# Routing weights stored as the last word of the residual rows, and five sets of expert weights in a fused attention and mixture-of-experts kernel

## The chip, the core and the metric

The kernel runs on one NeuronCore of a Trainium2 chip. Five engines work in parallel, each through its own instructions in order: TensorE (PE in the profile, with its weight loads as PEld), VectorE (DVE), ScalarE (ACT), GpSimd (POOL) and SyncE (SP), which here issues nearly all plain DMAs. Engines wait for each other and for DMAs through semaphores. SBUF is the on-chip memory of 128 partitions, PSUM holds TensorE's results, and HBM lies outside. The metric is the device time of one execution in microseconds (us); lower is better.

## The reference: what is computed

`x` is 2 x 1024 tokens of 256 features in float32. Four layers are added to it in turn, each on a layer norm of `x`:

```python
x = x + cross_attention(layernorm(x), ctx)     # 16 heads over 77 context rows
x = x + head_routed_attention(layernorm(x))    # the 4 best of 16 heads of each batch, 64 wide
x = x + gelu(layernorm(x) @ ctx.T) @ ctx       # per batch, 77 hidden units
x = x + moe(layernorm(x))

def moe(x):                                    # 8 experts, 256 -> 1024 -> 256, top 1
    probs = softmax(x @ w_router)
    sel, wgt = argmax(probs), max(probs)
    out = 0
    for e in range(8):
        y = relu(x @ w1[e] + b1[e]) @ w2[e] + b2[e]
        out = out + ((sel == e) * wgt)[:, None] * y
    return out
```

The change touches the last layer and the memory around it.

## The kernel before

**Tokens and stages.** The 2048 tokens lie as 16 tiles of 128 rows in one SBUF tile `xs`, which is the running `x`. Layers are called "a" (cross attention), "b" (the routed heads), "c" (gelu) and "d" (experts). Every engine's order is the order in which the program is written; `at(stage, step, position, f, ...)` hangs a piece of work on a step of `a_step` or `b_step`, and `piece` puts its copy out of PSUM off to the next step. Layers c and d of the first eight tiles run between the steps of the heads, those of the last eight in `b_end` and in `tail()`, whose `yield n` lets `n` pieces of the expert blocks run in between.

**The heads.** `b_step(i)` computes scores of one query tile against 1024 keys (L783), their maximum (DVE, L800) and exponential (ACT, L807). DVE transposes inside 32 x 32 squares (L813) and SP moves the squares with sixteen DMAs per pair of tiles (`beT<-be`, L835). PE multiplies by the values (L847), four steps later; DVE normalises (L876). The last pair of tiles turns on PE instead (L822).

**Routing.** `d_logits` gives eight logits per token, `d_expert` the best expert and running counts, `d_split` and `d_row` a token's place, `d_probability` the softmax weight of the chosen expert (subtract, exponential on ACT, sum, reciprocal) into `wgt`. Then `d_counts`, `d_blocks` (blocks of 128 rows per expert, and the expert of each block), `d_slots`, `d_tokens` and `d_lists` make the list of rows for each block. This is done twice: for the first eight tiles (five blocks, `K1`), during the heads, and for all the rest, in `tail()`.

**Rows through HBM.** `ztok` in HBM has one row of 513 words per token: 256 of the layer norm `y`, 256 of the residual `xs`, and the weight. `store_rows` stores the first two from SP for a pair of tiles (L337, L338). `store_weights` stores the weights of eight tiles as a column from ACT (L1101): 1,024 single words. `block_rows(n)` gathers a block's 128 rows with an indirect DMA of POOL (L1296) into `zb`, one of five buffers. A gather waits for the stores before it into `ztok`.

**A block.** `block_turn` transposes `y` on PE (`ybps`, L1308), ACT copies it (`ybT`, L1310) and POOL and DVE choose the bias; `block_hidden` runs the first layer (L1328) with relu on ACT (L1334); `block_out` the second (L1342), the bias (DVE, L1349), weight and residual (L1352), and POOL scatters the rows to `out` (L1355). Block `n + 1`'s hidden layer stands before block `n`'s output, and block `n + 2` is turned within it. Twenty blocks run.

**Weights.** `block_loads(n)` reads the expert's number from the table into SP (L1280) and loads `w1s`, `w2s`, `b2s` (L1282, L1286, L1290). There are four sets: one in pool `w0p`, laid on the left side of memory after step 22 of the heads, and three in `w1p`, on the right, where the heads' buffers `ebp` were. Block `n` takes the left set if `n % 4 == 0`. In the loop, block `n + 4` is asked for when block `n` begins; loads of the second table wait until it exists. `qk1`, which holds q, k and v of the second batch, stays to the end.

```python
wp = pools["w", min(n % 4, 1)]
...
next_loads.append(n + 4)
...
with nc.allow_non_contiguous_dma(reason="a column"):
    nc.scalar.dma_start(z[:, :, 2 * D], wgt[:, t0 : t0 + n])
```

Of the kernel before, what the change touches and what calls it, by code (L numbers as in the profile page):

```python
# [9 lines left out]
F32 = mybir.dt.float32  # L10
# [10 lines left out]
P = 128  # L21
# [18 lines left out]
def kernel(  # L40
# [30 lines left out]
    nc = tc.nc  # L71

    B, S, D = x.shape
# [3 lines left out]
    T = B * NT  # L77
# [19 lines left out]
    T1, K1 = 8, 5  # L97
# [14 lines left out]
    ytp = ctx.enter_context(tc.tile_pool(name="ytp", bufs=2, side="right"))  # L112
    ynp = ctx.enter_context(tc.tile_pool(name="ynp", bufs=3, side="right"))
    ap_ = ctx.enter_context(tc.tile_pool(name="ap_", bufs=2, side="right"))
    qk1 = ctx.enter_context(tc.tile_pool(name="qk1", bufs=1, side="right"))
    ybp = early.enter_context(tc.tile_pool(name="ybp", bufs=2))
    wsp = early.enter_context(tc.tile_pool(name="wsp", bufs=1))
    qk0 = early.enter_context(tc.tile_pool(name="qk0", bufs=1))
# [2 lines left out]

    xs = keep.tile([P, T, D], F32, name="xs")
    xv = x.rearrange("b (t p) d -> p (b t) d", p=P)
    ctxs = const.tile([KC, B, D], F32, name="ctxs")
    raw = {
# [203 lines left out]
            )  # L331
        return y

    def store_rows(t0, y_out):

        z = y_out[t0 * P : (t0 + 2) * P, :].rearrange("(t p) d -> p t d", p=P)
        nc.sync.dma_start(z[:, :, :D], rows["d", t0])  # L337
        nc.sync.dma_start(z[:, :, D : 2 * D], xs[:, t0 : t0 + 2, :])  # L338

    def add_bias(t0, n, bias):  # L340
        nc.gpsimd.tensor_tensor(
# [672 lines left out]
    oh = keep.tile([P, T, E], F32, name="eoh")  # L1014
    seen = keep.tile([P, T + 1, E], F32, name="eseen")
    nc.vector.memset(seen[:, 0, :], 0.0)
    wgt = keep.tile([P, T], F32, name="ewgt")
    emx = keep.tile([P, T], F32, name="emx")
    rkhi = keep.tile([P, T], F32, name="rkhi")
    rklo = keep.tile([P, T], F32, name="rklo")  # L1020
# [37 lines left out]
    def d_split(t0, n):  # L1058

        ts_ = slice(t0, t0 + n)  # L1060
        nc.vector.tensor_reduce(rkhi[:, ts_], ranks.pop(t0), AX.X, ALU.add)
        ri = small.tile([P, n], I32, name=f"eri_{t0}", tag=f"eri{n}")
        nc.vector.tensor_copy(ri, rkhi[:, ts_])
        nc.vector.tensor_scalar(ri, ri, P - 1, None, ALU.bitwise_and)
        nc.vector.tensor_copy(rklo[:, ts_], ri)
        nc.vector.tensor_tensor(rkhi[:, ts_], rkhi[:, ts_], rklo[:, ts_], ALU.subtract)
# [19 lines left out]
    def d_probability(t0, n):  # L1086

        ts_ = slice(t0, t0 + n)
        lg = logits[:, ts_, :]
        nc.vector.tensor_tensor(  # L1090
            lg, lg, emx[:, ts_].unsqueeze(2).to_broadcast([P, n, E]), ALU.subtract
        )
        nc.scalar.activation(lg, lg, AF.Exp)
        sm = small.tile([P, n], F32, name=f"esm_{t0}", tag="esm")
        nc.vector.tensor_reduce(sm, lg, AX.X, ALU.add)
        nc.vector.reciprocal(wgt[:, ts_], sm)

    def store_weights(t0, n):
        z = ztok[t0 * P : (t0 + n) * P, :].rearrange("(t p) d -> p t d", p=P)
        with nc.allow_non_contiguous_dma(reason="a column"):  # L1100
            nc.scalar.dma_start(z[:, :, 2 * D], wgt[:, t0 : t0 + n])  # L1101

# [171 lines left out]

    def block_loads(n):
        tab, i = table(n)
        wp = pools["w", min(n % 4, 1)]
        ex = nc.values_load(tab["eidi"][0:1, i : i + 1], engines=SP, min_val=0, max_val=E - 1)  # L1280
        w1s = wp.tile([P, C, F], F32, name=f"w1s_{n}", tag="w1s")
        nc.sync.dma_start(  # L1282
            w1s, w1.rearrange("e (c p) f -> p e c f", p=P)[:, bass.ds(ex, 1), :, :].squeeze(1)
        )
        w2s = wp.tile([P, FC, D], F32, name=f"w2s_{n}", tag="w2s")
        nc.sync.dma_start(  # L1286
            w2s, w2.rearrange("e (c p) d -> p e c d", p=P)[:, bass.ds(ex, 1), :, :].squeeze(1)
        )
        b2s = wp.tile([P, D], F32, name=f"b2s_{n}", tag="b2s")
        nc.sync.dma_start(b2s, b2[bass.ds(ex, 1), :].to_broadcast([P, D]))  # L1290
        ws[n] = (w1s, w2s, b2s)

    def block_rows(n):
        tab, i = table(n)
        zb = ybs[n] = pools["h"].tile([P, ZD], F32, name=f"zb_{n}", tag="zb", bufs=ZB)
        nc.gpsimd.indirect_dma_start(  # L1296
            out=zb[:, :],
            out_offset=None,
            in_=ztok[: T1 * P, :] if n < K1 else ztok[:, :],
            in_offset=bass.IndirectOffsetOnAxis(ap=tab["tok"][:, 0, i : i + 1], axis=0),  # L1300
        )
# [65 lines left out]
    def blocks():  # L1367


        block_turn(0)  # L1370
        block_turn(1)
        yield from block_hidden(0)
        for n in range(used):
            next_loads.append(n + 4)
            loads_due()
            if n + 1 < used:
                yield from block_hidden(n + 1)
            yield from block_out(n, n + 2 if n + 2 < used else None)
            next_rows.append(n + ZB)
            rows_due()  # L1380
# [15 lines left out]
    def every(gen):  # L1396
        for _ in gen:
            pass
# [7 lines left out]
    def at(stage, s, pos, f, *args):  # L1406
        plan.setdefault((stage, s, pos), []).append((f, args))
# [12 lines left out]
    def do_y(tag, t0, eng=nc.vector, store=True):  # L1420
        mv, rs, *y = rows[tag, t0]
        rows[tag, t0] = ln_rows(tag, t0, mv, rs, eng, *y)
        if tag == "d" and store:
            store_rows(t0, ztok)

    def do_rows(tag, t0, bias=None):

# [1 line left out]
        do_y(tag, t0, nc.gpsimd, False)  # L1429
        if bias is not None:  # L1430
            add_bias(t0, 2, bias)

    def store_rows_of(t0):
        store_rows(t0, ztok)

    def do_turn(tag, t0, pool=trp, ptag="tr", later=False):

# [102 lines left out]
    for g in range(3):  # L1540
        s, t0 = 4 * g, TG * g
        at("b", s + 10, 2, do_rows, "c", t0)
        at("b", s + 11, 3, piece, do_turn, "c", t0)
        at("b", s + 12, 3, c_hidden, t0)
        plan_gelu(t0, (s + 13, 0), (s + 13, 0), (s + 13, 2))
        at("b", s + 14, 2, piece, c_out, t0)
        at("b", s + 15, 2, do_rows_act, "d", t0)
        at("b", s + 17, 0, store_rows_of, t0)
        at("b", s + 17, 3, piece, do_turn, "d", t0)
    at("b", 18, 3, piece, d_logits, 0)  # L1550
    at("b", 22, 3, piece, d_logits, 2)
# [8 lines left out]
    plan_gelu(t0, (s + 2, 3), (s + 3, 0), (s + 3, 0))  # L1560
    at("b", s + 3, 2, piece, c_out, t0)
    at("b", s + 4, 2, do_rows_act, "d", t0)
    at("b", s + 5, 3, store_rows_of, t0)
    at("b", s + 5, 3, piece, do_turn, "d", t0)
    at("b", s + 6, 2, piece, d_logits, t0)

# [12 lines left out]
    def part(f, *args):  # L1579
        if f not in gens:  # L1580
            gens[f] = f(*args)
        next(gens[f], None)

    def first_weights():
        part(d_blocks)
        block_loads(0)
# [5 lines left out]


    at("b", 27, 3, d_row, 0, 4)
    at("b", 27, 3, d_probability, 0, 4)
    at("b", 28, 2, d_expert, T1 - 4, 4)
    at("b", 28, 3, lambda: due.append(d_counts(T1, 4)))
    at("b", 29, 2, d_split, T1 - 4, 4)
    at("b", 29, 3, d_probability, 4, 4)
    at("b", 29, 3, store_weights, 0, T1)  # L1600
    at("b", 30, 2, part, d_blocks, T1, K1)
    at("b", 30, 3, d_row, 4, 4)
    at("b", 30, 3, first_weights)
# [4 lines left out]

    def end_1():
        d_tokens(T1, K1)  # L1610
        store_rows_of(t2)
        do_turn("d", t2)

    def end_2():
# [16 lines left out]
    def tail():  # L1631

        do_turn("c", t4)
        yield 2
        do_y("c", t5)
        c_hidden(t4)
        do_power("d", t3)
        gelu(t4)
        yield 2
        do_turn("c", t5)  # L1640
        gelu(t4)
        d_expert(t2, 2)
        yield 2
        c_hidden(t5)
        gelu(t4)
        gelu(t5)
        yield 1
        c_out(t4)
        gelu(t5)
        gelu(t5)  # L1650
        yield 2
        do_power("d", t4)
        c_out(t5)
        do_y("d", t3, nc.gpsimd)
        yield 3
        do_power("d", t5)
        do_y("d", t4)
        yield 2
        do_turn("d", t3)
        do_y("d", t5)  # L1660
        yield 1
        do_turn("d", t4)
        yield 2
        d_logits(t3)
        d_expert(t3, 2)
        d_logits(t4)
        do_turn("d", t5)
        d_expert(t4, 2)
        yield 3
        d_logits(t5, t2, 4)  # L1670
        d_expert(t5, 2)
        d_split(t2, 4)
        yield 5
        evac = d_counts(T, 4)
        d_row(t2, 4)
        yield 1
        evac()
        d_split(t4, 4)
        yield 1
        d_probability(T1, T - T1)  # L1680
        store_weights(T1, T - T1)
        for _ in d_blocks(T, NB - K1):
            yield 2
        loads_due()
        d_row(t4, 4)
        yield 3
        for _ in d_slots(T, NB - K1):
            yield 2
        yield 3
        d_tokens(T, NB - K1)  # L1690
        yield 6
        d_lists(T, NB - K1)
        rows_due()

    with tc.manual_schedule(
# [41 lines left out]
        for s in range(NI):  # L1737
            b_step(s)
            if s == 0:
                a_step(T + 3)  # L1740
            if s == 22:
                early.close()
                pools["r", 0] = ctx.enter_context(tc.tile_pool(name="rp0", bufs=1))
                pools["w", 0] = ctx.enter_context(tc.tile_pool(name="w0p", bufs=1))
                pools["h"] = ctx.enter_context(tc.tile_pool(name="hp", bufs=2))
        b_end(end_1, end_2, end_3, end_4)
        stage_b.close()
        pools["w", 1] = ctx.enter_context(tc.tile_pool(name="w1p", bufs=3, side="right"))
        pools["r", 1] = ctx.enter_context(tc.tile_pool(name="rp1", bufs=1, side="right"))
        for n in range(1, 4):  # L1750
            block_loads(n)
        assert not plan, plan
        pieces = blocks()
# [55 lines left out]
```

## Time and profile before

| | |
|---|---|
| median of 3 runs | 565.71 us (565.46 to 566.82) |
| the profiled execution | 569.74 us |
| its span, first to last instruction | 568.0 us |
| mean granted TensorE clock | 0.966 |
| PE busy | 507.2 us (89%) |
| DVE, ACT, POOL busy | 319.4, 258.7, 195.0 us |
| moved by DMA | 94.33 MB, mean 166 GB/s |

The profile shows one execution. Its page cuts the span into 40 slices of 14.2 us; a digit is the busy share of an engine in tenths:

```profile
PE   3999999879889988899989889779898799999993
DVE  5558677861568977768867977845663111111111
PEclk9969999989987999999999999998999899999998
DMA  8100000020066668776876687578968999999900
```

Up to about 170 us the layer "a" runs, then the heads to about 390 us, and from there the expert blocks: PE is full, DVE nearly idle and the DMA engines busy. The blocks' first slices, near 390 to 450 us, still hold the second half's layers c and d.

In rows of the profile, `out<-in` names what an instruction writes and reads, `xN` how many there are, and `L1296` is a line of the kernel. A wait is put down to the releaser whose semaphore came last. A DMA has two times: its issue on the queue of an engine (SPq, ACTq, POOLq), and its landing. Matmul ends are modelled, and spans on POOL are rough.

### The profile page before, as it was taken

To read this page: it belongs to the slowest core of one execution; us is meant where nothing else is said; L and a number is where in the kernel's file an instruction comes from. 1 tells how busy PE (TensorE), PEld (TensorE's weight loads), DVE (VectorE), ACT (ScalarE), POOL (GpSimd) and SP (SyncE) were. 2 spreads that over 40 slices of the span, in tenths; PEclk is the share of its full clock that TensorE was granted. 3 is DMA by queue.
4 is the path that set the end of the run, shared out by engine and by line. 5 is a ranking of instruction groups with operands and counts; after the bars stand their busy time and mean duration, and the time that the engine had idled before them with its cause. 6 is when DMAs were issued, how large, how long until landed. Compare 5 with 4: busy or idle time off the path is not lost. (4 is left out here: it accounts for less than half of the span.)

```text
span 568.0 us, 11491 instructions
## 1 busy us (share of the span) xinstructions
PE 507.2 (89%) x4215; PEld 382.2 (67%) x4215; DVE 319.4 (56%) x702; ACT 258.7 (46%) x659; POOL 195.0 (34%) x281
## 2 busy tenths in 40 slices
PE   3999999879889988899989889779898799999993
PEld 2678777756445545567656565567798799999992
DVE  5558677861568977768867977845663111111111
ACT  3346666554443544447556665612423233333330
POOL 6647544643440012143432330424203233333211
PEclk9969999989987999999999999998999899999998
DMA  8100000020066668776876687578968999999900
GB/s 247 46 1 1 3 1 2 2 51 17 1 141 145 131 154 183 170 181 140 196 186 150 140 215 167 120 224 254 380 168 152 350 392 378 386 375 392 363 34 7
DMA packets 62500, 94.33 MB, mean 166 GB/s; under 512 B 16652, under 2 KB 47847, under 8 KB 62441
## 3 DMA queue, kind: packets, MB, share of 16 engines
q1 hardware_dynamic: 57092, 85.51, 53.8%
q0 software_dynamic: 2560, 7.35, 3.8%
q10 hardware_dynamic: 2789, 0.69, 0.8%
q8 instruction: 35, 0.57, 0.4%
q14 instruction: 24, 0.20, 0.1%
HBM read 55.77 MB, written 6.82 MB: 110 GB/s over the span
## 5 line engine op out<-in xcount | busy, mean ns | idle before, releaser
L807 ACT ACTIVATE be<-bsc,bnm 128x1024 f32<-128x1024 f32 x64 | 71.2, 1113 | 72.1 <-DVE bnm L800 61.0
L800 DVE TENSOR_REDUCE bnm<-bsc 128x1 f32<-128x1024 f32 x64 | 75.0, 1213 | 33.3 <-PE bsc L783 33.3
L783 PE MATMUL bsc<-kT,qT 64*128 64x512 f32 x256 | 73.8, 634 | 7.0 <-ACT be L807 7.0
L847 PEld LDWEIGHTS bov<-beT,v 128*64 128x64 f32 x1024 | 56.7, 139 | 33.1 <-issue 19.2
L1328 PEld LDWEIGHTS ph<-ybT,w1s 128*128 128x128 f32 x640 | 76.6, 194 | 1.8 <-ACT ybT L1310 0.3
L1328 PE MATMUL ph<-ybT,w1s 128*128 128x128 f32 x640 | 77.5, 278 | 0.0
L1342 PE MATMUL epo<-w2s,ehT 128*128 128x256 f32 x320 | 77.4, 386 | 0.0
L847 PE MATMUL bov<-beT,v 128*64 128x128 f32 x1024 | 64.7, 280 | 9.8 <-DMA beT<-be 6.8
L813 DVE STREAM_TRANSPOSE be<-be 128x1024 f32<-128x1024 f32 x60 | 71.2, 1223 | 2.2 <-DMA beT<-be 1.2
L1342 PEld LDWEIGHTS epo<-w2s,ehT 128*128 128x128 f32 x320 | 58.8, 194 | 6.6
L1334 ACT ACTIVATE ehT<-ph,b1s 128x128 f32<-128x128 f32 x120 | 32.6, 382 | 61.8 <-PE ph L1328 61.8
L1355 POOL DMA_INDIRECT out_dram<-ob,etok x20 | 20.5, 1027 | 103.3 <-DVE ob L1352 81.8
L783 PEld LDWEIGHTS bsc<-kT,qT 64*128 64x128 f32 x256 | 26.1, 191 | 38.3 <-issue 19.3
L1349 DVE TENSOR_TENSOR ob<-epo,b2s 128x256 f32<-128x256 f32 x20 | 8.5, 424 | 60.1 <-PE epo L1342 60.1
L496 DVE TENSOR_REDUCE mx<-sc 128x8 f32<-128x616 f32 x32 | 25.4, 793 | 24.0 <-PE sc L485 24.0
L517 ACT COPY eT<-pt 128x512 f32<-128x512 f32 (+1 forms) x48 | 23.4, 519 | 32.1 <-PE pt L516 32.1
L1320 DVE TENSOR_REDUCE b1s<-b1p 128x8 f32<-128x64 f32 x15 | 3.3, 220 | 49.6 <-POOL b1p L1315 49.6
L516 PE MATMUL pt<-ident,e 128*128 128x128 f32 x160 | 25.4, 292 | 1.5 <-ACT yT_a L1447 0.5
L498 DVE TENSOR_TENSOR e<-sc,mx 128x616 f32<-128x616 f32 x32 | 25.6, 799 | 1.9
L560 POOL TENSOR_TENSOR xs<-pa,xs 128x256 f32<-128x256 f32 x16 | 11.7, 730 | 37.5 <-ACT pa L559 37.5
L1296 POOL DMA_INDIRECT zb<-ztok,etok x20 | 19.6, 981 | 11.9 <-DVE ob L1352 6.4
L527 PEld LDWEIGHTS av<-vblk,eT 128*64 128x64 f32 x640 | 21.0, 143 | 3.3 <-issue 3.1
(283 smaller groups left out, 825.8 us busy)
## 6 DMA issues: line engine op xcount, KB each, us to landing
beT<-be SPq DMA_DIRECT2D x240, 128.0 KB, 2.4
w1s<-in_L_ffn_w_dram SPq DMA_DIRECT2D x20, 1024.0 KB, 9.5
w2s<-in_L_ffn_w_dram SPq DMA_DIRECT2D x20, 1024.0 KB, 10.4
b2s<-in_L_ffn_b_dram SPq DMA_DIRECT2D x20, 128.0 KB, 10.9
xs<-in_x_dram SPq DMA_DIRECT2D x4, 512.0 KB, 6.0
ztok<-y_d SPq DMA_DIRECT2D x8, 256.0 KB, 5.0
ztok<-xs SPq DMA_DIRECT2D x8, 256.0 KB, 6.2
ws_k<-in_L_ffn_Wk_dram SPq DMA_DIRECT2D x8, 64.0 KB, 2.0
```

The lines of the kernel that those rows point to most:

```text
L496: nc.vector.tensor_reduce(mx, scv, AX.X, ALU.max)
L498: nc.vector.tensor_tensor(em.rearrange("p (g h) k -> p g h k", g=2), scv, mx.unsqueeze(3).to_broadcast([P, 2, hb, KC]), ALU.subtract,)
L516: nc.tensor.transpose(pt[:, c - c0, :], e[:, off_c[c] : off_c[c] + P], ident)
L517: copy(eTs[t][:, c0 : c0 + n, :], pt[:, :n, :])
L783: nc.tensor.matmul(sc[h][:, n : n + 512], lhsT=qks[b, "q", m][r, q0 : q0 + P], rhs=qks[b, "k", m][r, n : n + 512], start=True, stop=True,)
L800: nc.vector.tensor_reduce(nm, sc[h], AX.X, ALU.max, negate=True)
L807: nc.scalar.activation(e, x, AF.Exp, bias=nm, accum_out=sms[g][:, q, s : s + 1])
L813: nc.vector.transpose(e, e)
L847: nc.tensor.matmul(o.rearrange("p (g x) -> p g x", g=QD) if i < LG else o, lhsT=vs[g * TG // NT][:, k, 2 * m + h, :], rhs=eT[:, :, q, h, k ...
L1328: nc.tensor.matmul(ph[:, f, :], lhsT=ws[n][0][:, c, f * P : (f + 1) * P], rhs=ybT[:, c, :], start=(c == 0), stop=(c == C - 1),)
L1334: nc.scalar.activation(hT[:, f, :], ph[:, f, :], AF.Relu, bias=b1s[:, f : f + 1])
L1342: nc.tensor.matmul(po, lhsT=hT[:, f, :], rhs=w2s[:, f, :], start=(f == 0), stop=(f == FC - 1))
```

## The change

Three things are changed together. **The weights** get their place as word 257 of each row of the residual's tile: `xs` becomes a view of `xw`, 257 words wide, and `wgt` its last column. The column stores are gone; `store_rows` stores `y` alone and a new `store_residual` stores residual and weight in one row of 257 words, once `d_probability` has run. That function becomes a generator with one stop after the exponential. **The sets** are five: two in `w0p`, three in `w1p`; block `n` takes the left pool if `n % 5` is 0 or 1, and block `n + 5` is asked for when block `n` begins. Block 1 is loaded in `end_1`, blocks 2 to 4 after the heads. **Memory**: `qk1` is closed after the heads, so that what is opened then on the right begins where q, k and v were; the blocks' small buffers `hp` go to the right, and the gathered rows `zb` get a pool `zp` of their own on the left.

```diff
-    qk1 = ctx.enter_context(tc.tile_pool(name="qk1", bufs=1, side="right"))
+    late = ExitStack()
+    qk1 = late.enter_context(tc.tile_pool(name="qk1", bufs=1, side="right"))
...
-    xs = keep.tile([P, T, D], F32, name="xs")
+    xw = keep.tile([P, T, D + 1], F32, name="xs")
+    xs, wgt = xw[:, :, :D], xw[:, :, D]
...
-    def store_rows(t0, y_out):
-
-        z = y_out[t0 * P : (t0 + 2) * P, :].rearrange("(t p) d -> p t d", p=P)
+    def store_rows(t0):
+
+        z = ztok[t0 * P : (t0 + 2) * P, :].rearrange("(t p) d -> p t d", p=P)
         nc.sync.dma_start(z[:, :, :D], rows["d", t0])
-        nc.sync.dma_start(z[:, :, D : 2 * D], xs[:, t0 : t0 + 2, :])
+
+    def store_residual(t0):
+
+        z = ztok[t0 * P : (t0 + 2) * P, :].rearrange("(t p) d -> p t d", p=P)
+        nc.sync.dma_start(z[:, :, D:], xw[:, t0 : t0 + 2, :])
...
-    wgt = keep.tile([P, T], F32, name="ewgt")
...
         nc.scalar.activation(lg, lg, AF.Exp)
+        yield
         sm = small.tile([P, n], F32, name=f"esm_{t0}", tag="esm")
         nc.vector.tensor_reduce(sm, lg, AX.X, ALU.add)
         nc.vector.reciprocal(wgt[:, ts_], sm)
-
-    def store_weights(t0, n):
-        z = ztok[t0 * P : (t0 + n) * P, :].rearrange("(t p) d -> p t d", p=P)
-        with nc.allow_non_contiguous_dma(reason="a column"):
-            nc.scalar.dma_start(z[:, :, 2 * D], wgt[:, t0 : t0 + n])
...
-        wp = pools["w", min(n % 4, 1)]
+        wp = pools["w", int(n % 5 > 1)]
...
-        zb = ybs[n] = pools["h"].tile([P, ZD], F32, name=f"zb_{n}", tag="zb", bufs=ZB)
+        zb = ybs[n] = pools["z"].tile([P, ZD], F32, name=f"zb_{n}", tag="zb", bufs=ZB)
...
-            next_loads.append(n + 4)
+            next_loads.append(n + 5)
...
+    def every_part(f, *args):
+        every(f(*args))
+
...
-    at("b", 27, 3, d_probability, 0, 4)
+    at("b", 27, 3, every_part, d_probability, 0, 4)
...
-    at("b", 29, 3, d_probability, 4, 4)
-    at("b", 29, 3, store_weights, 0, T1)
+    at("b", 29, 3, every_part, d_probability, 4, 4)
+    for s, t0 in ((29, 0), (29, 2), (30, 4), (30, 6)):
+        at("b", s, 3, store_residual, t0)
...
     def end_1():
         d_tokens(T1, K1)
-        store_rows_of(t2)
+        block_loads(1)
+        store_rows(t2)
         do_turn("d", t2)
...
         d_expert(t4, 2)
+        every(d_probability(t2, 4))
+        store_residual(t2)
+        store_residual(t3)
         yield 3
         d_logits(t5, t2, 4)
         d_expert(t5, 2)
+        weights = d_probability(t4, 4)
+        next(weights)
         d_split(t2, 4)
+        every(weights)
+        store_residual(t4)
+        store_residual(t5)
         yield 5
...
         yield 1
-        d_probability(T1, T - T1)
-        store_weights(T1, T - T1)
         for _ in d_blocks(T, NB - K1):
             yield 2
...
-                pools["w", 0] = ctx.enter_context(tc.tile_pool(name="w0p", bufs=1))
-                pools["h"] = ctx.enter_context(tc.tile_pool(name="hp", bufs=2))
+                pools["w", 0] = ctx.enter_context(tc.tile_pool(name="w0p", bufs=2))
+                pools["z"] = ctx.enter_context(tc.tile_pool(name="zp", bufs=2))
         b_end(end_1, end_2, end_3, end_4)
         stage_b.close()
+        late.close()
         pools["w", 1] = ctx.enter_context(tc.tile_pool(name="w1p", bufs=3, side="right"))
         pools["r", 1] = ctx.enter_context(tc.tile_pool(name="rp1", bufs=1, side="right"))
-        for n in range(1, 4):
+        pools["h"] = ctx.enter_context(tc.tile_pool(name="hp", bufs=2, side="right"))
+        for n in range(2, 5):
             block_loads(n)
```

More of the change, by code (lines that the diff above doesn't have):

```diff
@@ L1423, in do_y @@
         if tag == "d" and store:
-            store_rows(t0, ztok)
+            store_rows(t0)
     def do_rows(tag, t0, bias=None):
@@ L1431, in do_rows @@
             add_bias(t0, 2, bias)
-    def store_rows_of(t0):
-        store_rows(t0, ztok)
     def do_turn(tag, t0, pool=trp, ptag="tr", later=False):
@@ L1547 @@
         at("b", s + 15, 2, do_rows_act, "d", t0)
-        at("b", s + 17, 0, store_rows_of, t0)
+        at("b", s + 17, 0, store_rows, t0)
         at("b", s + 17, 3, piece, do_turn, "d", t0)
@@ L1562 @@
     at("b", s + 4, 2, do_rows_act, "d", t0)
-    at("b", s + 5, 3, store_rows_of, t0)
+    at("b", s + 5, 3, store_rows, t0)
     at("b", s + 5, 3, piece, do_turn, "d", t0)
```

## The prediction, made before the changed kernel was run

> **What bounds the kernel now.** The page's chain of waits covers only the last two per cent of the span, so I read the slices, then TensorE's (PE's) waits by window, then PE in order of time. The last stage, twenty expert blocks of 128 token rows, is PE without a gap. These are windows of exactly one block each (stretch; length, then busy us of PE, PE's weight loads, DVE, ACT, POOL; granted clock, DMA share, GB/s):
>
> ```profile
> 450.00:457.24 7.24, 7.24 (x51) 6.78 (x50) 1.13 (x3) 2.54 (x9) 2.15 (x3) 1.00 1.06 377
> 457.24:464.48 7.24, 7.24 (x51) 6.78 (x50) 1.13 (x3) 2.54 (x9) 2.61 (x4) 1.00 1.06 390
> ```
>
> PE is full at clock 1.00. A block's weights are 1024 + 1024 + 128 KB = 2.23 MB (the page's list of DMA issues); at 377 to 390 GB/s that is 5.7 to 5.9 us, below 7.24. So a faster load buys nothing here: the end comes earlier only by what PE loses before the steady part. PE's waits from 360 to 450 us name those losses (waiter <- releaser: total, times, longest):
>
> ```profile
> PE ybps L1308 <- DMA zb<-ztok,etok: 3.2, 1, 3.2
> ...
> PE bov L847 <- DMA beT<-be: 1.7, 1, 1.7
> PE tok L1229 <- DVE eblk L1219: 1.6, 1, 1.6
> ```
>
> The first is block 5, the first of the second list, whose rows come late from `ztok`. In order of time (start, length, what):
>
> ```profile
> 437.47 2.75 PE L1342 MATMUL epo<-w2s,ehT 128*128 128x256 f32 x12
> 443.44 0.44 PE L1308 MATMUL ybps<-ident,zb 128*128 128x128 f32 x2 [3.21 <-DMA zb<-ztok,etok]
> 443.71 1.56 PE L1342 MATMUL epo<-w2s,ehT 128*128 128x256 f32 x4
> 445.07 4.89 PE L1328 MATMUL ph<-ybT,w1s 128*128 128x128 f32 x32
> 449.80 2.75 PE L1342 MATMUL epo<-w2s,ehT 128*128 128x256 f32 x12
> ```
>
> This round, from one L1342 to the next, takes 449.80 - 437.47 = 12.33 us. The next (449.80 to 457.04) takes 7.24. The stall costs 12.33 - 7.24 = **5.09**: 3.21 of waiting, the rest in matmuls after it that run 1.56 for 1.03 and 4.89 for 3.73.
>
> Why are block 5's rows late? SP's waits from 365 us:
>
> ```profile
> SPq L1282 <- PE bov L847: 10.5, 1, 10.5
> SPq L1282 <- DMA ztok<-ewgt: 9.7, 1, 9.7
> ```
>
> and the stores into `ztok`, from 415 to 424 us (issue lengths in ns, then landings):
>
> ```profile
> L338 SPq DMA_DIRECT2D ztok<-xs x3: 360/467/735, 418.4 to 422.6; - x3
> L1101 ACTq DMA_DIRECT2D ztok<-ewgt x1: 449/449/449, 420.9 to 420.9; - x1
> ...
> DMA to landing us min/median/max: 6.8/10.0/13.9
> ```
>
> The column of weights is issued at 420.90 and lands at 434.80. In the trace's records the last residual store (issued 422.62) lands at 434.61, beside it. The lists are done on DVE near 429.5, but the gather of block 5 (POOL L1296), which must wait for every store into `ztok`, starts at 435.92 and lands at 443.39. SP's next weight load (block 5) also stands until 434.81, on the column itself.
>
> **The change, part by part.** The weight becomes word 257 of a residual row, so the 1,024-word column stores (L1101, two) go. The residual stores stay eight but are issued later, each after its weights.
>
> *Second half of the tokens: the stall before block 5.* Now `y` and residual stores come late because w2s of block 4 stands ahead of them on SP until block 0 is done (416.65). With five sets block 4 waits for nobody, and block 5 is asked for only once the second table exists. So `y` stores go out when made (about 404 to 409), residual pairs at about 413 and 418. A store 256 KB large lands 6.2 us after issue by the page (`ztok<-xs`); 418.5 + 6.2 = 424.7. (From 4.2 us, the store at 269.87, to 12.0, the one beside the column; I take 6.2, since the column is what is gone.) Then the lists decide: done 429.5 less 0.46 (below); POOL first scatters block 1's output (to 429.54 - 0.46 = 429.1) and needs 1.1 us from its last release to the gather, as from 434.82 to 435.92. Start: 430.2. Landing: the gathers in quiet took 3.6 to 3.8 us, under the weight stream 7.5, 7.9 and 9.3. Block 5's and 6's loads now start at about 424 and run beneath it, so I take 7.5: **437.7**, at worst 439.5. PE asks at 443.44 - 3.21 - 0.46 = 439.8. The stall goes, narrowly: margin 2.1 us, at worst 0.3. *A rule weighed here:* the Trainium skill, "DMA: Bandwidth & Descriptors", section on queues, rings and completion order, says each DMA engine takes turns between queues packet by packet. A gather of 263 KB would then get half of some 380 GB/s: an estimate of 3.7 + 263/190 - 263/380 = 4.4 us, margin 5. The rows say 7.5 to 9.3, and the rows decide; by either the stall goes. Gain **5.09**.
>
> *A second rule speaks against counting it all.* The Trainium skill, "TensorE: Matmul & The Clock Gate", section "Why this matters for your kernels", lets the clock fall to half only after PE gaps over about 3 us; so the 3.21 us wait costs the half clock and its end restores it. But the windows 385 to 390 and 410 to 415 show a granted clock of 0.66 and 0.67 after waits of only 1.3 us and less. By the rule no half-clock stretch would be left; by the row two are, and small shifts may make or remove one. A stretch lasts 3.4 us, so costs at most 1.7 us. I leave both as they are and put +-1.7 into the range.
>
> *DVE ahead of the lists (tok, 1.62).* DVE works without a break from 414.62 to 427.43. Probabilities leave that run: from 419.87 to 420.97, 1.10 with the wait for ACT. Their second half comes back earlier in the same run: subtract 0.22, sum 0.22, reciprocal 0.20 = 0.64, with ACT's exponential covered by the five instructions of `d_split`. The first half goes into DVE's idle 2.97 us before 414.62. Gain 1.10 - 0.64 = **0.46**. The exponential now stands before block 2's `ybT` copy on ACT (415.79, so about 0.7 later), which delays hidden 2 on PE; the remaining tok wait, 1.16, hides that. Without that cover it would cost 0.7.
>
> *First half of the tokens: the end of the heads.* Between 357.46 and 360.53, after the first of the last sixteen `beT` moves, SP stands still: the second needs the semaphore that the column (issued 355.17) holds. The page of waits puts 2.5 on it. The moves end 369.3 + 2.35 = 371.65, PE starts L847 at 371.70 after 1.70. Without the column all are 2.5 earlier, near 369.2, and PE is free at 370.0: gain **1.70**, and what follows (L847, L876, the first lists, POOL's bias product) hangs on it, so it carries. Two residual stores now precede those moves on SP. They wait for the reciprocal at 355.14 and take 2 x 0.5 us, and SP is idle until 357.46 anyway. The semaphores come round every eight DMAs, so moves 7 and 8 wait for their landing: 355.9 + 6.2 = 362.1 at worst, against an issue at 361.3: 0.8, still under the 0.8 of slack (369.2 to 370.0). Next late there is PE's own order.
>
> *Moved stores.* Four residual issues (0.5 each) leave SP between 269 and 340. Three precede idle time or DVE. The one before the moves at 341 could free the 0.57 that PE waits there; DVE is 9.01 busy of the 10 us after it, so 0.
>
> *Block 1's load in `end_1`* goes before `y` of t2 on SP. Three issues, 0.4 + 0.4 + up to 8 (the longest b2s issue); the `y` store behind it is needed by block 5 only, 40 us later. It takes 2.2 MB out of 388 to 403; no PE wait there is on weights. 0.
>
> *Memory.* Sets 2 to 4 lie over q, k, v of batch 1 and the heads' buffers, so SP's 10.5 us wait for the last L847 stays: that the heads' memory is given back gives no time itself. `hp` on the right is first written near 391, after the last L847 (388). 0.
>
> *Rows of 257 words.* DVE takes 799 ns for 616 elements in rows of 77 words (L498) and 690 for 512 in even rows (L995): 1.30 and 1.35 per element, no price for odd rows. Loads of `x` into odd rows: 0 to 0.5, taken 0.
>
> **Sum:** 5.09 + 0.46 + 1.70 = 7.25. The profiled execution was 569.74 with a span of 568.0; it becomes 562.5 and 560.8. The runs' median, 565.71, lies 4.0 under the profiled one; I take the gain off it: **558.5**.
>
> **Rivals.** *Half of it stays:* the column was only the last of several; the gather then ends in another wait (a slow residual store, its landing under two blocks' loads) and most of the 5.09 comes back. For it: three stores beside the column took 6.8 to 12 us. Against: they all shared 424 to 434. Time 565.71 - 1.70 - 0.46 = 563.6 if all comes back, 561 at half. *More than the sum:* one or two half-clock stretches fall away as well and the 0.57 counts: 558.5 - 1.7 - 1.7 - 0.6 = 554.5. *Slower, by the prefetch:* blocks 5 and 6 put 4.5 MB (12 us) on the DMA engines from 424, just under block 5's gather. PE then stands from 439.8 until it lands, plus 1.88 at half clock (5.09 - 3.21). To come out over 567.4, the stall must be over 7 us: landing after 446.8, 16.6 us after issue. At 18 us (448.2): 558.5 + 8.4 + 1.9 = 568.8. Against: 9.3 is the longest in the trace. *The change doing nothing* would need the gather to hang on none of these stores; its records name them.
>
> **How the numbers follow.** Forecast (556 to 561) 0.64; half stays (561 to 564) 0.20; more (554 to 556) 0.08; slower 0.05; nothing 0.03. A difference of 0.3% (1.7 us) is about what a measurement of this kernel can tell. Faster: 0.64 + 0.08 + 0.19 = 0.91 (0.01 of the half case ends nearer than that); within: 0.03 + 0.01 = 0.04; slower: 0.05. The range 555.0 to 563.5 leaves out some 2 in 10.
>
> **What would show it.** No `ztok<-ewgt`; the gather of block 5 issued near 428 (430.2 less the 1.70) and no PE wait of `ybps` on `zb`; the round from 437 at 7.24; L847 no longer waiting on `beT` near 371; clock 1.00 from then to the end. Wrong if the gather lands after PE asks, if SP's moves stand on residual stores, or if a new stretch at half clock takes the place.

## The result, and the profile after

The changed kernel takes **558.06 us** (median of 4 runs, 557.12 to 562.99) against 565.59 (4 runs, 565.29 to 566.82); the ratio is 0.987, 95% interval 0.983 to 0.991. The forecast was 558.5. In a repeat, taken with experiments 7 and 8, it took 563.50 against 569.23, ratio 0.990 (0.984 to 0.996). Ratios leave disturbed runs out and the medians beside them do not, so the two need not agree.

The profiled execution took 557.66 us, with a span of 555.9 and a granted clock of 0.977. That is 12.1 us under the profiled execution of before, more than the medians show; the surplus is dealt with at the end of this section. First the slices:

```profile
PE   3999999879879988899989899798899999999993
...
PEclk9999999989997999899999999899999999999998
DMA  8100000020067568875885787699977999999600
```

Each slice is now 13.9 us. Before, PE fell to 7 in two slices from 355 us and in one from 440, in which the stall before block 5 lay; of these one 7 is left, from 348 us, and from 403 us on PE is at 9. Next, PE's waits from 330 to 450 us (waiter <- releaser: total, times, longest):

```profile
PE bsc L790 <- ACT be L814: 2.7, 2, 2.1
PE po_b L890 <- DVE boT L883: 1.3, 1, 1.3
...
PE tok L1231 <- DVE eblk L1221: 0.5, 1, 0.5
```

The 3.2 us of `ybps` on `zb` and the 1.7 us of the values on `beT` are gone, and `tok` waits 0.5 for 1.6. In order of time around block 5 (start, length, what):

```profile
431.11 2.75 PE L1344 MATMUL epo<-w2s,ehT 128*128 128x256 f32 x12
433.70 0.38 PE L1310 MATMUL ybps<-ident,zb 128*128 128x128 f32 x2
433.92 1.03 PE L1344 MATMUL epo<-w2s,ehT 128*128 128x256 f32 x4
434.78 3.73 PE L1330 MATMUL ph<-ybT,w1s 128*128 128x128 f32 x32
438.36 2.76 PE L1344 MATMUL epo<-w2s,ehT 128*128 128x256 f32 x12
```

The round takes 438.36 - 431.11 = 7.25 us; it was 12.33. The repeat's trace agrees: block 5 is turned there at 443.98 without a wait, in a round of 7.25 us:

```profile
443.98 0.38 PE L1310 MATMUL ybps<-ident,zb 128*128 128x128 f32 x2
```

Back in the first trace, the stores into `ztok` from 395 to 430 us, and the gathers from 420 to 445 (issue lengths in ns, then first and last issue):

```profile
L345 SPq DMA_DIRECT2D ztok<-xs x4: 359/411/1166, 408.4 to 412.2; - x4
L340 SPq DMA_DIRECT2D ztok<-y_d x3: 375/548/604, 402.1 to 403.2; - x3
```

```profile
L1298 POOL DMA_INDIRECT zb<-ztok,etok x4: 963/966/1015, 423.5 to 438.6; - x4
...
DMA to landing us min/median/max: 6.4/7.2/7.9
```

Before, these stores left between 417.96 and 422.62. Now the last is out at 412.2, and the gather of block 5 is issued at 423.50 and lands at 431.38, 2.3 us before PE asks at 433.70.

**Where the surplus comes from.** In the clock records of all eleven traces the granted clock is whole or half, nothing between, so the time at half clock is 2 x span x (1 - mean clock): 2 x 568.0 x 0.034 = 38.6 us before, 2 x 555.9 x 0.023 = 25.6 after. It varies from execution to execution of the same kernel, from 21 to 58 us in 65 executions of before. The kernels ran in groups: A, B and C in the table, each on another chip, and the first four runs of the changed kernel, whose chip is not known. I fitted one level for each kernel, one shift for each group and one common slope to the 152 executions whose clock was recorded. The slope is 0.30 +- 0.03 us of time per us at half clock. (One slope for all is an assumption: fitted alone, it runs from 0.16 in experiment 1 to 0.47 in experiment 2.) The two profiled executions differ by 13.0 us at half clock, 4.0 us of time; 12.1 - 4.0 = 8.1 is left for the change.

At the same half clock, 25 us, the kernel before stands at 563.4 us in group A, 565.7 in B and 562.7 in C. So the groups differ by up to 3 us for one kernel, and each kernel is compared with the kernel before of its own group only. The last column does that at equal half clock; a minus means faster. Two kernels of different groups compare no better than through both differences.

| kernel (group) | median (range; runs), us | ratio to before (95%) | to before at equal half clock, us (95%) |
|---|---|---|---|
| before (A, B, C) | 566.5 (563.2 to 575.6; 65) | 1 | 0 |
| changed (first runs; repeat in B) | 560.8 (557.1 to 568.5; 10) | 0.987, 0.990 | -6.2 +- 1.2 (repeat) |
| 1 five sets alone (A) | 562.8 (558.8 to 564.5; 15) | 0.993 (0.990 to 0.995) | -2.6 +- 0.8 |
| 2 words alone (A) | 565.6 (555.5 to 572.5; 6) | 0.984 (0.977 to 0.992), on two of its six runs | -2.3 +- 1.1 |
| 3 words, no hold (C) | 560.8 (557.7 to 563.9; 12) | 0.991 (0.987 to 0.994) | -3.7 +- 0.9 |
| 4 column, no hold (C) | 564.7 (561.7 to 569.7; 12) | 1.000 (0.996 to 1.003) | -1.2 +- 0.9 |
| 5 first column back (A) | 562.7 (558.0 to 567.6; 19) | 0.993 (0.990 to 0.995) | -3.5 +- 0.7 |
| 6 probabilities late (A) | 555.05 (one run) | - | -5.4 +- 2.6 |
| 7 exponential earlier (B) | 555.0 (554.2 to 559.6; 6) | 0.979 (0.973 to 0.984) | -9.8 +- 1.3 |
| 8 and power later (B) | 554.0 (553.1 to 556.1; 6) | 0.975 (0.971 to 0.980) | -11.1 +- 1.3 |

### The profile page after: what moved, and what is told of

Same layout as the page of the kernel before. It is cut to its first block, busy times and chain, and to the rows that moved or that the text cites. A ratio compares the mean times of both kernels' runs of the same rounds, so it can differ in the third digit from the quotient of the medians.

```text
span 555.9 us, 11497 instructions
## 1 busy us (share of the span) xinstructions
PE 501.9 (90%) x4215; PEld 376.9 (68%) x4215; DVE 319.2 (57%) x705; ACT 259.0 (47%) x660; POOL 192.0 (35%) x281
## 5 line engine op out<-in xcount | busy, mean ns | idle before, releaser
L854 PEld LDWEIGHTS bov<-beT,v 128*64 128x64 f32 x1024 | 58.6, 143 | 30.6 <-issue 18.1
L1330 PEld LDWEIGHTS ph<-ybT,w1s 128*128 128x128 f32 x640 | 75.2, 192 | 2.4 <-ACT ybT L1312 1.3
L1344 PE MATMUL epo<-w2s,ehT 128*128 128x256 f32 x320 | 75.6, 380 | 0.0
L854 PE MATMUL bov<-beT,v 128*64 128x128 f32 x1024 | 66.7, 285 | 6.8 <-issue 2.0
L790 PEld LDWEIGHTS bsc<-kT,qT 64*128 64x128 f32 x256 | 25.9, 191 | 38.3 <-issue 18.6
L505 DVE TENSOR_TENSOR e<-sc,mx 128x616 f32<-128x616 f32 x32 | 25.6, 799 | 1.9
L523 PE MATMUL pt<-ident,e 128*128 128x128 f32 x160 | 24.3, 283 | 2.0 <-ACT yT_a L1446 1.0
L567 POOL TENSOR_TENSOR xs<-pa,xs 128x256 f32<-128x256 f32 x16 | 11.0, 686 | 38.6 <-ACT pa L566 38.6
L514 ACT ACTIVATE e<-e 128x616 f32<-128x616 f32 x32 | 21.5, 722 | 2.4 <-DVE e L505 2.4
```

The lines of the kernel that those rows point to most:

```text
L505: nc.vector.tensor_tensor(em.rearrange("p (g h) k -> p g h k", g=2), scv, mx.unsqueeze(3).to_broadcast([P, 2, hb, KC]), ALU.subtract,)
L523: nc.tensor.transpose(pt[:, c - c0, :], e[:, off_c[c] : off_c[c] + P], ident)
L790: nc.tensor.matmul(sc[h][:, n : n + 512], lhsT=qks[b, "q", m][r, q0 : q0 + P], rhs=qks[b, "k", m][r, n : n + 512], start=True, stop=True,)
L854: nc.tensor.matmul(o.rearrange("p (g x) -> p g x", g=QD) if i < LG else o, lhsT=vs[g * TG // NT][:, k, 2 * m + h, :], rhs=eT[:, :, q, h, k ...
L1330: nc.tensor.matmul(ph[:, f, :], lhsT=ws[n][0][:, c, f * P : (f + 1) * P], rhs=ybT[:, c, :], start=(c == 0), stop=(c == C - 1),)
L1344: nc.tensor.matmul(po, lhsT=hT[:, f, :], rhs=w2s[:, f, :], start=(f == 0), stop=(f == FC - 1))
```

## The experiments

The question was what made block 5's rows late. The prediction named the column of weights and, beside it, the load of block 4 that holds SP until 416.65 (called **the hold** here). The change removes both, so each was taken away without the other, in two ways.

### 1. Five sets alone; the column stays

```diff
-        wp = pools["w", min(n % 4, 1)]
+        wp = pools["w", int(n % 5 > 1)]
...
-            next_loads.append(n + 4)
+            next_loads.append(n + 5)
```

The rest of the memory's layout goes with it; words, `store_rows` and the column are those of before.

> The kernel before with the five sets and the memory of the change alone; weights stay a column. My theory (the column is slow only where it meets the row stores): the y and residual stores of the last tiles leave SP near 404 to 410 us, the column of the second half, issued near 420, runs nearly alone and lands in 5 to 7 us, the gather of block 5 starts near 430 and PE does not wait for it. The first half's stall on the column (1.7) and the 0.5 on DVE stay: 565.6 - 5.1 = 560.5. Rival (1,024 single words are slow by themselves, 13.9 us): it lands near 435, PE waits about 3 as before: 565.6.

Two `ztok` rows of its trace from 395 to 440 us, and block 5's turn in order of time:

```profile
L338 SPq DMA_DIRECT2D ztok<-y_d x3: 514/536/545, 402.0 to 405.5; - x3
...
L1102 ACTq DMA_DIRECT2D ztok<-ewgt x1: 372/372/372, 415.7 to 415.7; - x1
```

```profile
434.65 0.38 PE L1309 MATMUL ybps<-ident,zb 128*128 128x128 f32 x2
```

PE does not wait for the rows, with the column still there: issued at 415.72, it lands at 420.60 (by the semaphore records), in 4.9 us where it took 13.9. At equal half clock the time falls by 2.6 +- 0.8 us. So the column is not what makes rows late when the stores are out of its way.

### 2. Words alone; four sets stay

The reverse of experiment 1 on the changed kernel: its sets and memory are those of before.

> The kernel after with before's four sets and memory; the weights are words of the residual rows. My theory: the stores still stand behind block 4's second weights on SP until about 413 us, but without a column beside them the last lands within 8 us, before the lists are ready, so PE does not wait for block 5's rows: 558.5, as after. Rival (the four sets' hold on SP is what makes the rows late): the last store lands near 430 or later, PE waits 2 us or more for the rows, half clock follows: 561 to 563.

SP's waits from 330 to 450 us, the stores from 395 to 440, and block 5's turn:

```profile
SPq L1287 <- PE epo L1343: 17.5, 4, 14.5
```

```profile
L344 SPq DMA_DIRECT2D ztok<-xs x4: 359/676/927, 419.8 to 423.3; - x4
L339 SPq DMA_DIRECT2D ztok<-y_d x3: 371/468/947, 417.9 to 418.9; - x3
```

```profile
440.66 0.44 PE L1309 MATMUL ybps<-ident,zb 128*128 128x128 f32 x2 [1.16 <-DMA zb<-ztok,etok]
```

SP stands 14.5 us at block 4's second weights, and then sends seven stores of 256 or 257 KB, 1.8 MB in all, within 6 us. The last lands at 433.02, 9.7 us after its issue at 423.30, although no column runs beside it. The gather is issued at 433.83, and PE waits 1.16, where no wait was expected. The hold alone makes the rows late, by a third of what hold and column do together. At equal half clock the time falls by 2.3 +- 1.1 us, in which the gains of the words elsewhere are contained. PE has 10.2 us at half clock in this trace from 408.3 us on, but that is not what makes the rows late: the trace of experiment 4 has the same from 409.5 on, and no wait.

### 3 and 4. The hold taken away without a fifth set

If the hold is the cause, a fifth set is not needed: block 4's load has only to stand behind the stores on SP. One edit does that, to the kernel of experiment 2 (now 3) and to the kernel before (now 4). Block 4 is asked for when block 1 begins, not block 0.

```diff
         for n in range(used):
             next_loads.append(n + 4)
-            loads_due()
+            if n:
+                loads_due()
```

> Words in the rows, four sets, and block 4's load asked for one block later, so that on SP it stands behind the seven stores of y and residual. Theory (what made the rows late is the load of block 4 that held SP until 416.8, not the number of sets): the y stores leave near 402 to 406 and the residual ones by 414, the gather of block 5 is issued by 425, PE does not wait for zb at block 5 (the run with words and four sets alone waited 1.16), and the time at equal half-clock time is near that of the changed kernel, about 559. Rival (a fifth set is needed, since block 4's weights or block 5's load are late without it): a wait of PE of 1 us or more on zb, w1s or w2s between 420 and 450, and a time near 561 at equal half-clock time.

> The kernel before with that one edit: block 4's load behind the stores on SP; column and four sets stay. Theory (the hold made the stores bunch, and the bunch made the column slow): the column is issued near 416 and lands within about 5 us, the gather is issued near 424 to 425, PE does not wait for zb at block 5, and the time is 3 us under before, near that of five sets alone (560.6 at equal half-clock time). Rival (the column itself is the cause): it lands 10 us or more after its issue and PE waits 2 to 3.2 us on zb as before, time as before.

Experiment 3, stores from 395 to 440 us, and block 5's turn:

```profile
L344 SPq DMA_DIRECT2D ztok<-xs x4: 359/411/469, 410.2 to 415.7; - x4
L339 SPq DMA_DIRECT2D ztok<-y_d x3: 359/376/421, 403.2 to 404.6; - x3
L1297 POOL DMA_INDIRECT zb<-ztok,etok x3: 963/963/1012, 427.1 to 434.1; - x3
```

```profile
437.34 0.38 PE L1309 MATMUL ybps<-ident,zb 128*128 128x128 f32 x2
```

Experiment 4, the same:

```profile
L1101 ACTq DMA_DIRECT2D ztok<-ewgt x1: 372/372/372, 422.4 to 422.4; - x1
```

```profile
441.60 0.38 PE L1308 MATMUL ybps<-ident,zb 128*128 128x128 f32 x2
```

Neither waits for the rows: **a fifth set is not needed to take the wait away; moving one load does it.** (In experiment 3 the gather was issued at 427.1, not by 425, as its lists were done later there; it still came in time.) Whether the fifth set brings time beyond that is open. The ratios overlap (0.991 against 0.987 and 0.990). At equal half clock the changed kernel is 2.5 +- 1.5 us further under before than experiment 3, but in another group, and the traces do not show where: PE's waits from 330 to 450 us sum to 10.7 us in experiment 3 and to 9.9 in the repeat of the changed kernel.

Experiment 4 shows the column with the stores out of its way: issued at 422.37, six us later than expected, it lands at 427.44, in 5.1 us. The column queue's packets by window, first in the kernel before (420 to 424, then 424:428, 428:432, 432:434, 434:435; the first window has none), then in experiment 4 (420:424 and 424:425):

```profile
q10 hardware_dynamic: 651, 0.00, 27.6%
q10 hardware_dynamic: 361, 0.00, 20.3%
q10 hardware_dynamic: 23, 0.00, 2.7%
q10 hardware_dynamic: 5, 0.00, 0.3%
```

```profile
q10 hardware_dynamic: 674, 0.00, 8.8%
q10 hardware_dynamic: 366, 0.00, 20.6%
```

Both make 1,040 packets. By the trace's packet records, before they run from 424.40 to 434.10, at a mean of 30 ns a packet; in experiment 4 from 423.42 to 424.35, at 8.6 ns. The last stores suffer beside the column: 12.0 us to landing before, 9.7 in experiment 2, where the column is gone and the bunch stays. The same window of before, of experiment 2 and of experiment 3 (stretch; length, busy us of PE, PE's weight loads, DVE, ACT, POOL; clock, DMA share, GB/s) shows it:

```profile
428.00:432.00 4.00, 4.00 (x32) 3.79 (x30) 1.42 (x8) 1.52 (x7) 0.97 (x1) 1.00 1.01 100
```

```profile
428.00:432.00 4.00, 4.00 (x27) 3.72 (x27) 0.69 (x4) 2.17 (x8) 0.75 (x1) 1.00 1.12 206
```

```profile
428.00:432.00 4.00, 4.00 (x25) 3.46 (x24) 0.64 (x2) 2.43 (x9) 1.06 (x2) 1.00 1.06 379
```

Full DMA engines move 100 GB/s with stores and column, 206 with the bunched stores alone, and 379 where the stores are long done and weights stream.

Experiment 4's raw ratio shows no gain at all, against the expectation of 3 us. At equal half clock it is 1.2 +- 0.9 us under before, less than the 3.2 us of the wait; experiment 1, which also ends the wait and keeps the column, gave 2.6 +- 0.8. So the wait's end is certain, as the traces show it; its worth in time, without the words, is measured poorly.

### 5. The first half's column back

```diff
-        nc.sync.dma_start(z[:, :, D:], xw[:, t0 : t0 + 2, :])
+        w = D if t0 < T1 else D + 1
+        nc.sync.dma_start(z[:, :, D : D + w], xw[:, t0 : t0 + 2, :w])
...
     at("b", 29, 3, every_part, d_probability, 4, 4)
+    at("b", 29, 3, store_weights, 0, T1)
```

> The kernel after with the first eight tiles' weights stored as a column from ACT again. My theory: SP stands about 2.5 us on the column's semaphore after the first of the last sixteen moves, PE waits about 1.7 for beT: 558.1 + 1.7 = 559.8. Rival (the heads' end is bound by DVE and ACT and the 1.7 does not carry): 558.1, with a PE wait of the same size elsewhere in the kernel after.

PE at the end of the heads, in order of time:

```profile
359.27 4.00 PE L796 MATMUL bsc<-kT,qT 64*128 64x512 f32 x8 [2.14 <-ACT be L820]
363.19 3.68 PE L860 MATMUL bov<-beT,v 128*64 128x128 f32 x32
...
372.10 1.97 PE L860 MATMUL bov<-beT,v 128*64 128x128 f32 x32
```

The moves were held for the column until 359.31, as before, yet PE starts on the last values at 372.10 without a wait. A stretch at half clock (3.68 for 1.97 in the second row) had made PE late first. So the expected wait did not come in this trace. At equal half clock the kernel is 2.7 +- 1.4 us slower than the changed one, of another group, where 1.7 was expected. The four traces with this column agree: without a stretch here PE waited 1.7 (before) and 1.4 (experiment 4), with one 0.4 (experiment 1) and 0 (this one).

### 6. The second half's probabilities back in their old place

```diff
-        every(d_probability(t2, 4))
-        store_residual(t2)
-        store_residual(t3)
...
         yield 1
+        every(d_probability(T1, T - T1))
+        for t0 in (t2, t3, t4, t5):
+            store_residual(t0)
```

> The kernel after with the second half's probabilities computed in their old place, after the last counts, and its residual rows stored there. My theory: DVE's run from the last logits to the block lists is 0.5 us longer and PE's wait of tok on eblk goes from 0.5 to about 1.0; the stores land by about 424 and the rows of block 5 are in time: 558.6. Rival (early stores are needed): PE waits for block 5's rows, 561 or more.

From 395 to 450 us PE waited:

```profile
PE tok L1231 <- DVE eblk L1221: 1.5, 1, 1.5
```

1.5 for 0.5: without the move PE waits 1 us longer for the lists. The 0.3 us that the changed kernel waits for `ybT` is gone here, so the move is worth 0.7 to 0.8 us of waiting, more than the 0.46 that was counted for it. One execution can't place the time to better than 2.6 us.

### 7 and 8. A version that beats both

PE's largest wait left before the blocks is that of the scores for ACT, 2.1 us near 357. Experiment 7 asks for the exponential of tiles 4 to 7 one step of the heads earlier; experiment 8 also moves layer c's power for `t4` from the end of `end_2` to the start of `end_3`. The changed kernel was run again beside them.

```diff
-    at("b", 29, 3, every_part, d_probability, 4, 4)
+    halves = d_probability(4, 4)
+    at("b", 28, 3, next, halves, None)
+    at("b", 29, 3, next, halves, None)
...
         c_hidden(t3)
-        do_power("c", t4)
 
     def end_3():
+        do_power("c", t4)
```

> The kernel after, with the first half of the probabilities of tiles 4 to 7 (subtract and exponential) one step earlier, at step 28 of the heads. In the kernel before DVE stands 1.97 us there for ACT's exponential, which is behind four activations; the transposes, the maxima of the last scores and the last moves are behind it. Theory (this is now the end of the heads): DVE does not wait, PE's 2.1 us wait of bsc on be falls to under 0.5, the moves start up to 2 us earlier: 558.1 - 1.7 = 556.4. Rival (ACT sets that place): the wait moves to ACT, 558.1.

> As x5, and the layer norm sums of tiles 12 and 13 go behind the normalisation of the last but one query tile on DVE, so that PE's 1.3 us wait of po_b on boT falls. Theory: another 1.1: 555.3. Rival (what was moved is needed at once by the layers behind it): the wait comes back at y_c, as x5.

> The kernel after, unchanged, beside x5 and x6 on the same chip: 558, with a spread of some us between runs. Theory for the spread: stretches of half clock of 3.4 us fall differently in each run, and time rises by about 0.45 us for each us at half clock. Rival (the spread comes from DMA): time does not follow the mean granted clock.

PE's waits of experiment 8 from 330 to 450 us:

```profile
PE bpt L829 <- ACT beT L832: 1.1, 1, 1.1
...
PE ybps L1310 <- DMA zb<-ztok,etok: 0.6, 1, 0.6
PE bsc L790 <- ACT be L814: 0.6, 1, 0.6
```

and two windows of the changed kernel, then of experiment 8:

```profile
350.00:360.00 10.00, 7.76 (x49) 4.41 (x50) 7.38 (x19) 6.84 (x24) 3.99 (x8) 0.81 0.53 129
360.00:370.00 10.00, 9.54 (x82) 6.97 (x81) 6.28 (x19) 4.62 (x9) 2.07 (x5) 0.84 0.87 195
```

```profile
350.00:360.00 10.00, 9.88 (x76) 5.09 (x76) 9.62 (x25) 7.92 (x26) 4.95 (x10) 1.00 0.74 178
360.00:370.00 10.00, 8.55 (x92) 7.25 (x89) 6.30 (x21) 4.28 (x8) 1.49 (x3) 1.00 0.88 214
```

The wait falls from 2.1 to 0.6 us, and part of it comes back at `bpt`, 1.1 for 0.2, as the rival had it. All of PE's waits from 330 to 450 us sum to 7.2 us, in experiment 7 to 8.3 and in the changed kernel's repeat to 9.9. Over the 20 us of the windows PE is busy for 18.4 us at full clock, where it was busy for 17.3 with a clock of 0.81 and 0.84. Experiment 7 is 3.6 +- 1.5 us under the changed kernel of its group at equal half clock, experiment 8 another 1.3 (less than its uncertainty), as PE's 1.3 us wait of `po_b` is gone too and 0.6 comes back at block 5. They also spend less time at half clock: 25.9 and 24.3 us on average, against 39.2 in the changed kernel and 38.5 in the kernel before beside them. Experiment 8 is the fastest, 553.96 us: 2.5% (2.0 to 3.0) under before. The repeat of the changed kernel gave 563.50 (560.14 to 568.54), far from the 558 expected. Most of that is half clock, 39.2 us on average against 28.2 in the first runs: at 25 us the two stand at 559.5 and 558.1. The expected slope was 0.45 us per us at half clock; it is 0.30.

## Why the prediction was right

**The stall before block 5 (5.09).** Right in size and in its mechanism's end: gather in time, no wait, round of 7.25. The margin, put at 2.1 us, was 2.3. (The gather's issue, 423.50, and PE's turn, 433.70, both came some 4.5 us earlier than forecast, as this execution had spent 20.5 us at half clock by then, and before 30.7.) The gather took 7.88 us under the weight stream; 7.5 was taken from the rows of before, against an estimate of 4.4 by the packet turns of the Trainium skill's page "DMA: Bandwidth & Descriptors", section on queues, rings and completion order. By 4.4 the margin would have been 433.70 - 423.50 - 4.4 = 5.8; the row was right. The cause was weighted wrongly, in one step: the residual store was sized at 6.2 "since the column is what is gone". The column is not what decides. Gone alone it leaves 1.16 us of waiting and a store that lands after 9.7 us (experiment 2); kept, without the hold, it lands in 4.9 and 5.1 us and nothing waits for the rows (experiments 1 and 4). The hold bunches the stores, and a column in the bunch makes the last of them slower. The forecast stood because the change removes both. The rival that half stays was thus the true case for the words alone, with a third of the wait.

**Half clock in that 5.09.** The 1.88 us behind the stall were half clock, and the sum counted on their end. At equal half clock, which leaves that part out, the sum is 3.21 + 0.46 + 1.70 = 5.4, and the repeat gives 6.2 +- 1.2 us. Whether the 1.88 come in full is open: the time at half clock was 39.2 us in the repeat and 38.5 in the kernel before beside it, within the scatter. "A stretch lasts 3.4 us" was too short: the eleven traces, the last stretch of each left out, have 51 of 3.4, 6.8 or 10.2 us, and 24 of them are longer than 3.4. The sign of being wrong, a new stretch at half clock, did come, though not in the same place twice: the changed kernel's first trace has one of 6.8 us from 356.3, where before has none, and lacks the two near 385 and 410; its second has three, of 6.8, 3.4 and 10.2 us, from 361.5, 392.3 and 412.7. That it left the forecast standing was luck.

The second rule weighed, that the clock falls to half only after gaps over about 3 us (the Trainium skill, "TensorE: Matmul & The Clock Gate", section "Why this matters for your kernels"), is too lax in this case. Of PE's idle gaps in the eleven traces, the first 30 and the last 20 us left out, these were followed by half clock within 3.5 us: all 22 of 2.6 to 2.9 us (two places in each trace), 11 of 30 of 1.9 to 2.5, 7 of 68 of 1.3 to 1.9, none of 65 of 0.8 to 1.3. At the wait near 357 it was six of the nine traces in which PE waits 2.1 us; in the two where the wait is 0.6 or less there is none.

**The end of the heads (1.70).** Right in mechanism; its size stays open. The hold of the moves is gone (they leave from 354.44 to 363.88 without a stop) and so is the wait. Putting the column back costs 2.7 +- 1.4 us at equal half clock, through two groups, but in that kernel's own trace nothing waits, as a half-clock stretch there hides it.

**The probabilities (0.46).** Their leaving DVE's run shortened it from 12.81 to 12.24 us, 0.57. PE's wait for the lists fell by more, from 1.6 to 0.5, and 0.3 came back in front of the hidden layer of block 2, for `ybT`, as the prediction had named it. Experiment 6 puts the whole at 0.7 to 0.8.

**Costed at nothing, rightly so far as the trace shows:** the heads' memory (SP still waits 6.0 us for the last values before block 2's load), block 1's load in `end_1`, rows of 257 words and the stores moved ahead of `beT`: no PE wait on any of them appears. *Slower by the prefetch* needed the gather to land 16.6 us after issue; it took 7.9.

That the first median lies 0.4 us from the forecast is luck: those runs happened to have little half clock, 28.2 us on average. In the repeat, with 39.2, the median was 563.50, at the edge of the stated range, while the kernel before took 569.23 beside it.

## What to carry to other kernels

When a row of small stores is late, look at what stands ahead of it on its queue before blaming the slowest of them: one load that waits for a buffer bunched seven stores here, and moving that load took the wait away as an added buffer did. A wait that is gone in the trace is worth its length only if nothing else makes the waiter late as often. Compare kernels at equal granted clock, and in one group of runs, before a difference of 1% is believed.

## What the runs showed of the hardware

- Executions of one kernel spend from 21 to 58 us at half clock, and each us costs 0.30 +- 0.03 us of time. This makes most of the scatter: the correlation of time with it is 0.83 over 65 executions of the kernel before and 0.99 over ten of the changed one.
- At equal half clock the kernel before stood at 563.4, 565.7 and 562.7 us in three groups of runs, each on another chip.
- Between a trace's first and last record, stretches at whole and at half clock last whole multiples of 3.41 us, in all eleven traces. Gaps of PE of 2.6 to 2.9 us were always followed by half clock (22 of 22), gaps of 1.9 to 2.5 us in 11 of 30.
- The same 1,024 single words to HBM take 0.7 us of packets when the queues are free (experiment 1: 416.63 to 417.32) and 9.7 us among row stores. Full DMA engines move 100 GB/s then, and 206 with the row stores alone (428 to 432 us).
